# Joined query products carried one group further, into the seventh sequence of an eight-sequence attention and expert block

## The chip, the cores and the metric

The kernel runs on one core of one Trainium2 chip. The metric is device time in microseconds (us) of one execution; several executions are given by their median. Five engines work side by side, each in its own program order: PE (TensorE, matrix products), DVE (VectorE), ACT (ScalarE), POOL (GpSimd) and SP, which here only issues DMAs. They wait for each other through semaphores.

## What is computed

The input x holds 8 sequences of 512 rows of 256 numbers, all in float32. The block is

```python
x = x + _layernorm(_L0_attn_ref(_layernorm(x), wq, bq, wkv, bkv, wo))
x = x + _layernorm(_L0_ffn_ref(_layernorm(x), ...))
```

The attention has 4 groups of 4 query heads (head size 128), each group with one key and one value head, a sinusoidal position table added to queries and keys, a causal mask and a softmax. The second half is a mixture of 64 experts (6 per row, at most 64 rows for an expert) with a shared expert beside it. The queries of one group of one sequence, which the change is about, are

```python
q = (x @ wq + bq).reshape(b, t, G, QPG, D).transpose(0, 2, 3, 1, 4)
q = q + pe
```

so for one group a product of 512 x 256 rows with 256 x 512 weights.

## The kernel before

The attention is a loop over `k` from 0 to 127, here called *places*. Place k belongs to sequence b = k // 16 and, in it, to slot s = k % 16; four places make a group. The sequences are counted from 0 in the code, so the seventh sequence is b = 6, whose places are 96 to 111, and the sixth sequence's slot 11 is place 91. The order of the instructions on every engine is the order in which the program writes them (a manual schedule), so one late instruction holds up everything behind it on its engine.

At each place PE makes four blocks of scores (L566; at most three lie in PSUM at a time, in the pool `ps_s`), DVE masks them and takes their minimum (L570), ACT takes the exponential (L574), DVE the reciprocal of the sums (L580), and POOL scales the weights with it (L584, `weigh`). One place later DVE transposes the weights in blocks (L602, `turned`), four DMAs write them to HBM (`ex_d`, L606) and one reads them back in another order (`et`, L612). Two places after the scores, `mix` multiplies them with the values (L639), and ACT brings the result out (`ao`, L650). Projections of earlier places run between these (`projections`, L664 or, in sequences 1 to 5, sums of blocks: `cross` on POOL, L707 to L710, whose result `across` multiplies at L716). Keys and values of the next group are made at L377 and L388. The rows of the sequences b = 1 to 6 are transposed through HBM, and POOL sorts them into `xnt` (L364, `sort`).

Queries are made in two ways. `queries(k)` (L426, result added up at L431) makes two heads of half of a group's rows in four products of 256 columns; a group takes four such calls, sixteen products, and eight DVE instructions. Groups 2 to 23 (group = 4 b + g) are instead made in pairs by seven products of summed blocks for what eight plain ones would give: `ask(k)` (four products, L490 to L493), `answer` (one), `ask_rest` (one) and `ask_fourth` (one), all recorded at L470. They take from POOL four sums of the weights (`join_heads`, once for each group of heads, at the start) and four sums of the rows (`join_rows`, L459 to L462, once per sequence, into the one tile `rows_joined`), and eight DVE instructions for each `ask`, sixteen a group (L496, L497, L505, L510, L515). `ask(k)` runs at even k for the group k // 4 + 1, two calls a group, and its parts are spread over places k, k + 1 and k + 2. Its two PSUM banks come from the pool `ps_m` of three; the bank `back` is given up only at place k + 2, by `answer_fourth`. Which groups are made so is decided by `in_pairs`:

```python
def in_pairs(k):
    return k % 2 == 0 and JOINED_FROM <= k // QPG + 1 < JOINED_TO
```

and the plain way begins where it ends:

```python
asked_for = {2: (4, 5), 3: (6,), 4: (7,)}.get(k, (k + 2,) if JOINED_TO * QPG <= k + 2 < NK else ())
```

So before the change `queries(96)` to `queries(99)`, for group 24, run at places 94 to 97, and `queries(100)` at place 98. The tile that takes the queries is tagged `qt` in the plain way, and in the pairs `qt` for odd groups and `rows` for even ones.

From place 94 on the experts run beside the attention (`routed`): first a table is built (`tables`, DVE sorting steps at L804 and L806 and two small products, L883 and L895), from place 97 on rows are gathered by POOL (L948) and weights loaded by DMAs that ACT issues (L958, L965). Place 97 also has `combine`, six POOL sums (L744 to L749), and place 98 `cross(47)` and `across(47)`.

## Time and profile before

| what | number |
|---|---|
| three executions | 1351.22, 1346.76, 1350.15 us, median 1350.15 |
| the profiled execution | 1346.28 us |
| its span on the core | 1344.6 us, so 1.7 us lie around it |
| PE busy | 1319.8 us, 98% of the span |
| DVE, POOL, ACT busy | 911.5, 660.3, 546.8 us |
| granted clock of PE | 0.997 of full speed |
| plain query products, L426 | 40 calls of `queries`, 8 records of 379 ns each |
| joined query products, L470 | 44 calls of `ask`, 14 records each |

A product of float32 is two records on PE, so four products of `queries` are eight records. The records overlap: one of 256 columns is listed at 379 ns, while the next starts about 217 ns after it (4 records in 0.87 us, 8 in 1.73 us). The start-to-start time is what a product costs in a stream, and "busy" alone does not tell whether PE is held up. Times "at" a number are us from the start of the span. Place 92 has its scores at 841.63, place 93 at 852.44, then 859.99, 868.56, 876.96, 884.62 (place 97), 894.16 (place 98) and 906.60 (place 99).

### The profile page before, as it was taken

What the parts mean: (1) busy time and instruction counts of PE and PEld (TensorE: products, weight loads), DVE (VectorE), ACT (ScalarE), POOL (GpSimd) and SP (SyncE); (2) the same over time, 40 slices, a digit from 0 to 9 for tenths busy, and PEclk for the clock granted to TensorE, in tenths of its full rate; (3) what the DMA queues carried; (4) which work ended last, traced back from release to release, by engine and by line L of the source; (5) the groups of instructions that cost most, each with busy time, mean ns of one, the idle gap of its engine ahead of it and who ended that gap; (6) DMA issues with size and microseconds to landing.
All of it is one profiled execution on the core that took longest, in us unless ns stands there. A gap on an engine that the chain in (4) does not pass through costs nothing. (4 is left out here: it accounts for less than half of the span.)

```text
span 1344.6 us, 21778 instructions
## 1 busy us (share of the span) xinstructions
PE 1319.8 (98%) x6746; PEld 1018.7 (76%) x6746; DVE 911.5 (68%) x2931; ACT 546.8 (41%) x1665; POOL 660.3 (49%) x1080
## 2 busy tenths in 40 slices
PE   9999999999999999999999999999999999999997
PEld 7877887888778887788778877876667676767774
DVE  5575577777887678777886778666656444567645
ACT  3333354334443454344433443434343334444523
POOL 4556463436452563446434643355545444477711
PEclk9999999999999999999999999999999999999999
DMA  8676677756775676566765667579999889777712
GB/s 268 176 219 208 201 215 219 205 185 211 220 218 174 201 226 213 177 209 204 224 193 162 204 189 202 171 213 303 307 284 281 246 239 299 182 239 262 234 36 72
DMA packets 160435, 285.53 MB, mean 212 GB/s; under 512 B 17292, under 2 KB 123437, under 8 KB 160317
## 3 DMA queue, kind: packets, MB, share of 16 engines
q1 hardware_dynamic: 122893, 212.14, 52.6%
q0 software_dynamic: 13328, 36.05, 9.1%
q10 hardware_dynamic: 24096, 35.92, 8.5%
q8 instruction: 55, 0.90, 0.3%
q14 instruction: 63, 0.52, 0.1%
HBM read 168.44 MB, written 115.61 MB: 211 GB/s over the span
## 5 line engine op out<-in xcount | busy, mean ns | idle before, releaser
L584 POOL TENSOR_SCALAR e<-e,recip 128x512 f32<-128x512 f32 (+1 forms) x504 | 245.3, 525 | 424.1 <-DVE recip L580 367.7
L574 ACT ACTIVATE e<-e,least 128x32 f32<-128x32 f32 (+1 forms) x504 | 258.5, 514 | 260.4 <-DVE least L570 235.1
L639 PE MATMUL pav<-et,v 128*128 128x256 f32 x1280 | 300.4, 382 | 11.5 <-DMA et<-ex_d 8.9
L639 PEld LDWEIGHTS pav<-et,v 128*128 128x128 f32 x1280 | 241.5, 191 | 52.8 <-issue 7.1
L566 PE MATMUL psc<-kt,qt 128*128 128x32 f32 (+15 forms) x1024 | 274.9, 407 | 0.9 <-DVE qt L431 0.4
L570 DVE CUSTOM_DVE_ANT_0 e<-psc,mask 128x32 f32<-128x32 f32 (+1 forms) x504 | 204.2, 430 | 96.4 <-PE psc L566 93.8
L650 ACT ACTIVATE ao<-pav,bv_sb 128x256 f32<-128x256 f32 x255 | 107.1, 471 | 368.5 <-PE pav L639 344.7
L566 PEld LDWEIGHTS psc<-kt,qt 128*128 128x128 f32 x1024 | 161.5, 191 | 59.4 <-issue 25.9
L602 DVE STREAM_TRANSPOSE eb<-e 128x1024 f32<-128x1024 f32 (+1 forms) x252 | 197.5, 822 | 2.0 <-POOL e L584 1.5
L1021 POOL DMA_INDIRECT y_d<-dd,idx x32 | 51.1, 1597 | 93.2 <-ACT e L574 27.2
L574 ACT ACTIVATION_READ_ACCUMULATOR e<-e,least 128x1 f32 x504 | 94.6, 188 | 0.0
L716 PEld LDWEIGHTS pc<-set,crossed 128*128 128x128 f32 x640 | 77.0, 192 | 4.9 <-issue 1.7
L716 PE MATMUL pc<-set,crossed 128*128 128x128 f32 x640 | 78.8, 276 | 0.6 <-POOL crossed L710 0.6
L426 PE MATMUL pq<-xnt,wq_sb 128*128 128x256 f32 x320 | 75.5, 380 | 0.0
L716 PEld LDWEIGHTS ps<-set,ao 128*128 128x128 f32 x480 | 59.9, 192 | 15.3 <-issue 7.4
L470 PE MATMUL pq_back<-rows_joined,heads 128*128 128x256 f32 x264 | 71.3, 379 | 0.0
L388 PEld LDWEIGHTS pv<-wkv_sb,xnt 128*128 128x128 f32 x512 | 65.9, 192 | 4.5 <-issue 1.1
L388 PE MATMUL pv<-wkv_sb,xnt 128*128 128x128 f32 x512 | 67.5, 275 | 0.5 <-ACT ao L650 0.5
L426 PEld LDWEIGHTS pq<-xnt,wq_sb 128*128 128x128 f32 x320 | 59.2, 190 | 9.2 <-issue 0.7
L379 DVE SCALAR_TENSOR_TENSOR kt<-pk,bk_sb,pe_sb 128x512 f32<-128x512 f32 x32 | 24.0, 750 | 60.5 <-PE pk L377 58.5
L470 PEld LDWEIGHTS pq_back<-rows_joined,heads 128*128 128x128 f32 x264 | 50.2, 190 | 16.2 <-issue 8.2
L377 PE MATMUL pk<-xnt,wkv_sb 128*128 128x512 f32 x128 | 60.2, 593 | 0.3 <-ACT xnt L120 0.3
(281 smaller groups left out, 2017.6 us busy)
## 6 DMA issues: line engine op xcount, KB each, us to landing
ex_d<-eb SPq DMA_DIRECT2D x504, 160.0 KB
et<-ex_d SPq DMA_DIRECT2D x126, 640.0 KB
wgu<-in_w_gate ACTq DMA_DIRECT2D x32, 352.0 KB
wgu<-in_w_up ACTq DMA_DIRECT2D x32, 352.0 KB
wd<-in_w_down ACTq DMA_DIRECT2D x32, 352.0 KB
set<-wc_d SPq DMA_DIRECT2D x20, 512.0 KB
set<-ws_d SPq DMA_DIRECT2D x20, 384.0 KB
y<-y_d POOLq DMA_DIRECT2D x10, 512.0 KB, 6.8
```

What stands on the lines that cost most here:

```text
L377: nc.tensor.matmul(pk, lhsT=wkv_sb[:, c, g, 0, :], rhs=s["xnt"][:, c, :], start=c == 0, stop=c == NC - 1)
L388: nc.tensor.matmul(pv[:, i, :], lhsT=s["xnt"][:, c, ts(2 * n + i, P)], rhs=wkv_sb[:, c, g, 1, :], start=c == 0, stop=c == NC - 1, skip_gro ...
L426: nc.tensor.matmul(pq[:, n, :, :], lhsT=wq_sb[g][:, c, ts(2 * pair + n, D)], rhs=seqs[b]["xnt"][:, c, :].rearrange("p (u v) -> p u v", v=P ...
L470: nc.tensor.matmul(out, lhsT=factor[0], rhs=factor[1], start=first, stop=last, skip_group_check=True)
L566: nc.tensor.matmul(psc[:, :w], lhsT=halves[k // 2][:, at, :, :].rearrange("d h t -> d (h t)"), rhs=seqs[b]["kt"][g][:, :w], start=True, st ...
L570: nc.vector.tensor_tensor_reduce(out=e, in0=psc[:, :w].rearrange("p (c t) -> p c t", t=BS), in1=mask[:, T - w :].rearrange("p (c t) -> p c ...
L574: nc.scalar.activation(e, e, AF.Exp, bias=l["least"][:, q : q + 1], scale=-1.0, accum_out=l["total"][:, q : q + 1])
L584: engine.tensor_scalar(e, e, recip[:, q : q + 1], 1.0, ALU.mult, ALU.mult)
L602: nc.vector.transpose(eb[:, :, first : first + count, :, :].rearrange("p a j r t -> p j a r t"), weighed[k % 2][:, end - count : end, :, : ...
L639: nc.tensor.matmul(pav[n // NI][:, :, n % 2, :], lhsT=seqs[b]["v"][g][:, j, :], rhs=et[:, :, first + j, :], start=j == 0, stop=j == count ...
L650: nc.scalar.activation(ao, pav[n // NI][:, :, n % 2, :], AF.Identity, bias=bias)
L716: nc.tensor.matmul(bank_[:, n, :], lhsT=a, rhs=w, start=pair == 0 and n == 0, stop=pair == 1 and n == len(factors[0]) - 1, skip_group_chec ...
```

## The change

The bound of the joined groups goes from 24 to 25, and `join_rows` is called at slot 11 of the sixth sequence (b = 5) too.

```diff
-JOINED_FROM, JOINED_TO = 2, (EARLY + 1) * G
+JOINED_FROM, JOINED_TO = 2, (EARLY + 1) * G + 1
...
-            if k == 2 or s == 11 and b < EARLY:
+            if k == 2 or s == 11 and b <= EARLY:
                 join_rows(b + 1 if s == 11 else 0)
```

With EARLY = 5 and G = 4 the first line reads 2, 25. The calls `queries(96)` to `queries(99)` at places 94 to 97 go. `ask(92)` comes at place 92 (behind the projection there) and `ask(94)` at place 94 (in front of `weigh`, as at every even place of the sixth sequence but 92), with their answers at places 93 to 96. The four POOL sums of the seventh sequence's rows come at the end of place 91. The queries of group 24 lie in tiles tagged `rows` instead of `qt`; `load_whole_again` takes a `rows` tile at place 98. The sums of the weights that group 24 reads lie in tiles tagged `wgu` and `wd`, into which the experts' weights are loaded from places 97 and 98 on. No DMA is added, removed or moved in the program's order, and no line number changes.

## The prediction

> **What bounds the kernel now.** I read the page first. PE is busy in every slice, and the granted clock is 0.997, so the kernel ends when PE has worked through its stream; a change counts by what it does to that stream.

> ```profile
> PE 1319.8 (98%) x6746; PEld 1018.7 (76%) x6746; DVE 911.5 (68%) x2931; ACT 546.8 (41%) x1665; POOL 660.3 (49%) x1080
> PE   9999999999999999999999999999999999999997
> ```

> "Busy" has modelled ends, so next I read the timeline of PE at places 94 to 98, start to start (start, duration, engine, line, operation, count, and in brackets the idle time before it and what ended it).

> ```profile
> 872.18 1.89 PE L426 MATMUL pq<-xnt,wq_sb 128*128 128x256 f32 x8
> 873.91 2.32 PE L639 MATMUL pav<-et,v 128*128 128x256 f32 x10
> ...
> 888.56 1.89 PE L426 MATMUL pq<-xnt,wq_sb 128*128 128x256 f32 x8
> 890.28 2.32 PE L639 MATMUL pav<-et,v 128*128 128x256 f32 x10
> ...
> 897.49 1.89 PE L426 MATMUL pq<-xnt,wq_sb 128*128 128x256 f32 x8
> 900.00 2.05 PE L716 MATMUL pc<-set,crossed 128*128 128x128 f32 x16 [0.61 <-POOL crossed L710]
> ```

> The reader is to see two things. One call of `queries` costs 873.91 - 872.18 = 1.73 us. And PE runs without a gap from place 92 on until 900.00, where it waits for POOL. So I read POOL there:

> ```profile
> 889.77 1.89 POOL L584 TENSOR_SCALAR e<-e,recip 128x448 f32<-128x448 f32 x4 [6.16 <-DVE recip L580]
> 891.83 1.08 POOL L948 DMA_INDIRECT gx<-xg_d,idx  x1 [0.17 <-issue]
> 892.94 0.46 POOL L744 TENSOR_TENSOR o<-partial 128x128 f32<-128x128 f32 x1
> ...
> 896.01 1.00 POOL L948 DMA_INDIRECT gx<-xg_d,idx  x1
> 897.03 0.74 POOL L707 TENSOR_TENSOR crossed<-ao 128x256 f32<-128x256 f32 x1
> ...
> 899.22 0.73 POOL L710 TENSOR_TENSOR crossed<-ao,crossed 128x256 f32<-128x256 f32 x1
> ```

> From 889.77 to 899.95 POOL has 10.2 us of work without a pause: `weigh(97)`, a gather, the six sums of `combine`, a gather, `cross(47)`. It starts from DVE's reciprocal, which follows the scores of place 97 (884.62). So PE's product at 900.00 stands 15.38 us behind the scores of place 97 by POOL's chain, whatever PE does in between, as long as that is less. This is the heart of the forecast.

> **PE's own work.** Removed: four `queries`, 4 x 1.73 = 6.92 us, one each at places 94 to 97. Added: where the fifth sequence does the same an `ask` takes 1.73 us (697.17 to 698.90) and each of its three later products 0.43 (for instance 710.37 to 710.80); 1.73 + 3 x 0.43 = 3.02, twice 6.04 us. By place: 92 +1.73; 93 +1.29; 94 none (1.73 for 1.73); 95 1.29 - 1.73 = -0.44; 96 and 97 each -1.73. If every record counted: 6.04 - 6.92 = -0.9 us. Until the scores of place 97, however, all of the new work is done and only three of the four removals: 6.04 - 5.19 = **+0.85**. The fourth, at 888.56, lies inside POOL's 15.38 us. Removing it lets PE come 1.73 us earlier to a place where it waits already, so the wait of 0.61 becomes about 2.3 (1.4, if item 4 below takes its part) and the end does not move.

> **Waits that the change adds before place 97.** Between 841 and 899 PE has no idle time that could be filled or freed, so none of these can be below zero.

> 1. Place 92 to 93. DVE gets the four instructions of `ask` in front of its sorting steps (L804, L806): 0.42 + 0.42 + 0.48 + 0.42, spaced 0.33 apart in the earlier slots, about 1.65 us from 851.35. The sorting then ends near 855.65, while the moved scores of place 93 come at 854.17; the fourth score block needs the first one's bank, which DVE frees near 855.9, at PE's 855.85. Cost 0.1 (0 to 1.0, the whole lag of DVE).
> 2. Place 94. `pm` (L883) now takes the third PSUM bank beside the two of `ask(94)`, so `mix(92)` waits until DVE has emptied `front`. There this is 2.22 us after the first product (697.17 to 699.39); PE arrives after 1.73 + 0.26 = 1.99. Cost 0.25 (0 to 0.5, the wait of PE for ACT in front of L388 near 800).
> 3. Place 96. The landing marks put `et` of place 94 at 880.23, 11.67 us after the scores of place 95; PE will want it 8.40 - 0.44 + 3.45 = 11.41 us after them. Cost 0.25 (0 to 1.8, the longest wait for an `et` near by, at 929.5).
> 4. Place 97. `et` of place 95 lands at 887.81, 10.85 us after the scores of place 96. PE wants it at 13.32 now and at 13.32 - 2 x 1.73 = 9.86 then: a wait of 1.0 us, but it lies inside POOL's 15.38 (4.9 + 2.2 + 1.7 + 2.0 + 1.3 + 1.7 = 13.8 us of PE). Cost 0.

> So the scores of place 97 come 0.85 + 0.1 + 0.25 + 0.25 = about **1.5 us later**, and all behind them with them.

> **At no cost, and their cover.** POOL's four sums: 4 x 0.72 = 2.9 us at the end of place 91, from 836.92, where POOL sits idle 4.21 us until `ao` at 841.13. The fourth must wait for a product at 840.31 to 840.7 that reads the old sum, so `cross(44)` starts some 0.6 late; its reader is PE at 854.33, ten us on. Without that cover they would cost 2.9. DVE's sixteen instructions for eight are 16 x 0.44 - 8 x 0.475 = +3.2 us in five places whose DVE is 51 to 88% busy; beyond items 1 and 2 the waits of DVE for PE in front of each place (0.98 at 860.20, 0.82 at 869.14) take them. No queue gets a new DMA. The reload into `rows` at place 98 waits for scores of place 97, by then done; the weight tiles tagged `wd` are reloaded at 907.73, 30 us behind their last new reader.

> [...]

> **Behind place 98.** The experts' loads are issued by ACT behind `mix(95)`, which comes about 0.7 us earlier in its place than before. PE's next waits are for `et`, 1.80 at 929.52 and 1.00 at 944.25, amid a DMA share of 0.98. They could vanish (-2.8) or double (+2.8). I take 0: loads and exchange move together.

> **The sum.** 1346.28 + 1.5 = 1347.8 for the profiled execution. That one lies 3.9 us below the median of the three runs, so the forecast for the median is 1350.15 + 1.5 = **1351.7**.

> **The rivals.**

> *A, every record counts.* POOL's chain gives way: the gathers or `combine` start earlier, or the 0.61 was chance. Then -0.9: 1349.3. For it speaks that PE is 98% busy; against it the unbroken POOL rows. With the two `et` waits gone, too, 1346.5.

> *B, slower: the exchange falls behind the weight stream.* From 906 on each place loads over 2 MB of weights; an `et` that landed 3.9 us after issue at 883.94 took 7.0 at 922.34. If the shifted loads get ahead of the exchange, the two waits double: 1.5 + 2.8 = +4.3, 1354.5. It decides once an `ex_d` or `et` is issued behind one more 0.7 MB pair of loads than now. For it: the DMA share; against it: the loads are issued in place order and the `et` of place 96 begins to land at 896.3 and is wanted at 901.89.

> *C, DVE sets the pace at 92 to 96.* Items 1 and 3 at their upper ends: 0.85 + 1.0 + 0.5 + 1.8 = +4.15, 1354.3, by gaps before 885. Against it: DVE's idle time in front of every place.

> **Chances.** Forecast 0.62, A 0.2, B 0.12, C 0.06. What a measurement can tell from no change is 0.3%, 4.05 us; the four executions lie between 3.9 below and 1.1 above the median. B and C lie just past 4.05 (0.14 of their 0.18), and scatter adds 0.03 from the forecast: slower 0.17. Scatter takes A below -4.05 rarely (0.04) and the forecast more rarely (0.02): faster 0.06. The rest, 0.77, is no change. The range goes from A with its waits gone to B and C with a little scatter: 1346.3 to 1355.

> **What would show it.** Right: no L426 record between 863 and 897; POOL's L707 at place 98 still ends an unbroken row that began at L584; in front of that `pc` a PE wait of 1.3 to 2.3 us instead of 0.61; a wait of about 1 us for `et` at place 97; the scores of place 97 some 1.5 us later. Wrong: that `pc` less than 15 us behind the scores of place 97 (A), `et` waits over 4 us in sum between 905 and 950 (B), PE gaps over 2 us in sum before place 97 (C).

## The result, and the profile after

The changed kernel took 1353.35 us in the median of seven runs (1350.99 to 1357.57), the kernel before 1346.89 beside it (seven, 1345.42 to 1351.22): a ratio of 1.0045 [1.0027, 1.0062], some 6 us slower. In a second comparison with more runs (the first experiment) it was 1.003 [1.0014, 1.0046], 4 us. The forecast was +1.5 us, a ratio of 1.0011, which both intervals exclude. The predicted range held the time, and the direction of the sum was right; its size was not, and the loss stands at or just over the 0.3% that was called no change (a greater loss had been given 0.17). That the time itself came within 1.7 us of the forecast 1351.7 is luck: the three runs of the kernel before on which that rests had a median 3.3 us above that of the seven, from which the same sum gives 1348.4, 5 us short of what was measured.

The profiled execution of the changed kernel is its slowest one: 1357.57 us, span 1355.7, granted clock 0.993. A profile of the same kernel taken later has a span of 1349.2. Wherever a number below hangs on one execution, both are given.

The page of the changed kernel, PE's row and its 40 slices:

```profile
PE 1325.1 (98%) x6742; PEld 1022.1 (75%) x6742; DVE 914.1 (67%) x2939; ACT 546.3 (40%) x1665; POOL 662.9 (49%) x1084
PE   8999999999999999999999999999999999999997
```

PE has four records less (6746 - 32 + 28) and is as busy as before: still the engine that sets the end.

**Up to place 98.** The timeline of PE, places 94 to 98 of the changed kernel:

```profile
867.57 1.03 PE L470 MATMUL pq_front<-xnt,wq_sb 128*128 128x256 f32 x4
...
869.89 2.40 PE L639 MATMUL pav<-et,v 128*128 128x256 f32 x10 [0.16 <-PE pm L883]
...
887.20 2.31 PE L566 MATMUL psc<-kt,qt 128*128 128x96 f32 x8
889.35 1.95 PE L716 MATMUL pc<-set,crossed 128*128 128x128 f32 x16
892.37 2.43 PE L639 MATMUL pav<-et,v 128*128 128x256 f32 x10 [1.08 <-DMA et<-ex_d]
...
902.57 2.05 PE L716 MATMUL pc<-set,crossed 128*128 128x128 f32 x16 [0.99 <-POOL crossed L710]
```

No L426 stands between 863 and 897 any more. At place 97 (scores at 887.20) PE waits 1.08 us for `et`, and at place 98 again 0.99 us for POOL; that is what removing `queries(99)` bought. (Removing `queries(98)`, which lies ahead of these scores, did count: the shift of the scores falls from 3.41 at place 96 to 1.97 at place 97.) POOL there:

```profile
892.35 1.89 POOL L584 TENSOR_SCALAR e<-e,recip 128x448 f32<-128x448 f32 x4 [4.72 <-DVE recip L580]
894.40 1.08 POOL L948 DMA_INDIRECT gx<-xg_d,idx  x1 [0.17 <-issue]
895.51 0.46 POOL L744 TENSOR_TENSOR o<-partial 128x128 f32<-128x128 f32 x1
...
898.59 1.00 POOL L948 DMA_INDIRECT gx<-xg_d,idx  x1 [0.16 <-issue]
899.61 0.74 POOL L707 TENSOR_TENSOR crossed<-ao 128x256 f32<-128x256 f32 x1
...
901.79 0.73 POOL L710 TENSOR_TENSOR crossed<-ao,crossed 128x256 f32<-128x256 f32 x1
```

The row is as unbroken as before, 10.2 us from 892.35 to 902.52, and PE's `pc` starts at its end: 15.37 us behind the scores of place 97, where it was 15.38. The wait in front of it, 0.99, is below the 1.3 to 2.3 that the forecast gave as a sign: the wait for `et` at place 97 and the slower start of the products behind it (`pc` and `mix` took 5.29 us from their start to that of `pk`, where they had taken 1.79 + 2.16) took about 1.3 of the 1.73 us and left 0.4. The scores of place 99 come at 909.17 instead of 906.60. Place 90 already lies 0.61 us later in this execution, for reasons ahead of the change, so the change itself is worth +1.97 there, and +2.05 in the second profile of the same kernel.

**Behind place 98** the two profiles part. The view of PE's waits, 905 us to 1340 us (total, times, longest), first before, then after:

```profile
PE pav L639 <- DMA et<-ex_d: 8.0, 6, 2.8
```

```profile
PE pav L639 <- DMA et<-ex_d: 11.3, 6, 2.9
```

PE waits for the same thing in both kernels, the exchange of weights, and some 3 us longer after. The same view of the later profile gives 8.9 in 5 waits, only 0.9 more than before, although its span is 4.6 us longer than that of before. So there is a cost that the waits do not show. The windows of the changed kernel (start and end, length, busy us and records of PE, of its weight loads, DVE, ACT, POOL, then the granted clock, DMA share, GB/s):

```profile
1185.00:1195.00 10.00, 10.00 (x42) 7.58 (x42) 6.85 (x25) 3.19 (x10) 8.23 (x14) 1.00 0.92 306
1195.00:1205.00 10.00, 7.21 (x29) 5.82 (x28) 5.47 (x21) 1.75 (x6) 6.49 (x11) 0.83 0.93 310
1268.00:1275.50 7.50, 5.18 (x26) 3.45 (x24) 4.11 (x16) 1.64 (x5) 5.54 (x10) 1.00 0.77 224
1275.50:1283.00 7.50, 6.90 (x18) 5.54 (x19) 1.84 (x10) 2.26 (x6) 2.09 (x4) 0.55 0.54 199
```

and two products of its timeline there:

```profile
1200.34 4.10 PE L639 MATMUL pav<-et,v 128*128 128x256 f32 x10 [2.79 <-DMA et<-ex_d]
...
1276.10 4.61 PE L639 MATMUL pav<-et,v 128*128 128x256 f32 x10 [2.92 <-DMA et<-ex_d]
```

The ten records take 4.10 and 4.61 us instead of 2.43 at 892.37. The clock column says why: in the two stretches that hold them, behind waits of 2.79 and 2.92 us, the granted clock was 0.83 and 0.55; it was 0.5 for 3.41 us from 1200.35 and for 6.83 us from 1275.44. The kernel before has the first of the two (0.83 from 1195 to 1205); in its profile the waits near 1270 are 0.38 and 0.82 us, and the granted clock from 1268 to 1276 was 1.00:

```profile
1195.80 3.95 PE L639 MATMUL pav<-et,v 128*128 128x256 f32 x10 [2.78 <-DMA et<-ex_d]
...
1268.72 2.40 PE L639 MATMUL pav<-et,v 128*128 128x256 f32 x10 [0.38 <-DMA et<-ex_d]
...
1275.50 2.43 PE L639 MATMUL pav<-et,v 128*128 128x256 f32 x10 [0.82 <-DMA et<-ex_d]
```

### The profile page after: what moved, and what is told of

Its sections match the earlier page's. It is cut to its first block, busy times and chain, and to the rows that moved or that the text cites. A ratio compares the mean times of both kernels' runs of the same rounds, so it can differ in the third digit from the quotient of the medians.

```text
span 1355.7 us, 21785 instructions
## 1 busy us (share of the span) xinstructions
PE 1325.1 (98%) x6742; PEld 1022.1 (75%) x6742; DVE 914.1 (67%) x2939; ACT 546.3 (40%) x1665; POOL 662.9 (49%) x1084
## 3 DMA queue, kind: packets, MB, share of 16 engines
q1 hardware_dynamic: 122893, 212.14, 52.7%
q0 software_dynamic: 13328, 36.05, 8.9%
## 5 line engine op out<-in xcount | busy, mean ns | idle before, releaser
L584 POOL TENSOR_SCALAR e<-e,recip 128x512 f32<-128x512 f32 (+1 forms) x504 | 245.2, 525 | 425.4 <-DVE recip L580 367.2
L639 PE MATMUL pav<-et,v 128*128 128x256 f32 x1280 | 304.6, 386 | 15.8 <-DMA et<-ex_d 12.8
L639 PEld LDWEIGHTS pav<-et,v 128*128 128x128 f32 x1280 | 244.4, 193 | 57.9 <-issue 10.2
L716 PEld LDWEIGHTS pc<-set,crossed 128*128 128x128 f32 x640 | 77.0, 192 | 4.8 <-POOL crossed L710 1.4
L716 PE MATMUL pc<-set,crossed 128*128 128x128 f32 x640 | 78.9, 277 | 1.0 <-POOL crossed L710 1.0
L470 PE MATMUL pq_back<-rows_joined,heads 128*128 128x256 f32 x276 | 74.6, 379 | 0.0
L716 PEld LDWEIGHTS ps<-set,ao 128*128 128x128 f32 x480 | 59.9, 192 | 15.3 <-issue 6.9
L388 PEld LDWEIGHTS pv<-wkv_sb,xnt 128*128 128x128 f32 x512 | 65.9, 192 | 4.5 <-issue 1.1
L388 PE MATMUL pv<-wkv_sb,xnt 128*128 128x128 f32 x512 | 67.5, 276 | 0.5 <-ACT ao L650 0.5
L426 PE MATMUL pq<-xnt,wq_sb 128*128 128x256 f32 x288 | 67.8, 379 | 0.0
L716 PE MATMUL ps<-set,ao 128*128 128x128 f32 x480 | 60.1, 275 | 0.0
```

The source lines that it names most:

```text
L388: nc.tensor.matmul(pv[:, i, :], lhsT=s["xnt"][:, c, ts(2 * n + i, P)], rhs=wkv_sb[:, c, g, 1, :], start=c == 0, stop=c == NC - 1, skip_gro ...
L426: nc.tensor.matmul(pq[:, n, :, :], lhsT=wq_sb[g][:, c, ts(2 * pair + n, D)], rhs=seqs[b]["xnt"][:, c, :].rearrange("p (u v) -> p u v", v=P ...
L470: nc.tensor.matmul(out, lhsT=factor[0], rhs=factor[1], start=first, stop=last, skip_group_check=True)
L584: engine.tensor_scalar(e, e, recip[:, q : q + 1], 1.0, ALU.mult, ALU.mult)
L639: nc.tensor.matmul(pav[n // NI][:, :, n % 2, :], lhsT=seqs[b]["v"][g][:, j, :], rhs=et[:, :, first + j, :], start=j == 0, stop=j == count ...
L716: nc.tensor.matmul(bank_[:, n, :], lhsT=a, rhs=w, start=pair == 0 and n == 0, stop=pair == 1 and n == len(factors[0]) - 1, skip_group_chec ...
```

## The experiments

There were twelve runs. "Local shift" is when the scores of place 99 come against the profile of before, with the offset at place 90 taken off. The theories in the expectations go by letters. In short: S blames the tiles in which group 24's queries lie; M is the forecast, a local delay carried to the end one for one; D is a delay that grows on its way; E places the extra loss at places 118 to 127, where the exchange meets the reading back of `y` for the last step of the earlier sequences; F places it at 98 to 102, among the experts' weight loads.

**1. The changed kernel again (`after_again`).** No edit.

> The changed kernel unchanged, for a second profile. Theory M (about 2 us are made at places 92 to 97 by PE's own work, the moved waits and POOL's chain; the rest comes behind place 98, where a wait for et that grows past about 2.5 us is followed by 3.4 us at half the PE clock): the scores of place 98 again 1.5 to 2.0 us late against their position in the kernel before, counted from place 90; the waits for et at places 100 to 102 differ from the first profile; ratio 1.003 to 1.006. Theory S (the other tiles for the queries of group 24 change later waits for good): the same, but with the extra time behind place 98 at the same places and of the same size as in the first profile.

Measured: 1354.06 us (twelve runs, 1348.31 to 1358.49) beside 1349.38, ratio 1.003 [1.0014, 1.0046]; local shift +2.05. The loss and the local shift are real. The wait of 2.46 us at 947.03 in the first profile did not come again.

**2. The kernel before again (`before_again`).** No edit.

> The kernel before unchanged, for a second profile and to see how its waits behind place 98 vary. Theory M: waits for et at other places or of other sizes than in the first profile, by 1 to 3 us; ratio 0.998 to 1.002. Theory S: the same waits within 0.5 us.

Measured: 1348.68 us, 0.9995 [0.9983, 1.0008]; no local shift (0.01), but 1.89 us earlier at place 102. So places 100 to 103 move by some two microseconds from run to run without any edit, and one profile cannot tell there.

**3. Only the tiles (`tag_only`).** The kernel before, with the queries of group 24 in the tiles that the change gives them.

```diff
-halves[half] = p2.tile([D, 2 * NI, QPG, BS], F32, tag="qt", name=f"qt_{half}")
+halves[half] = p2.tile([D, 2 * NI, QPG, BS], F32, tag="rows" if half in (48, 49) else "qt", name=f"qt_{half}")
```

> The kernel before, the queries of group 24 made the plain way but put into tiles tagged rows as in the change. Theory M: ratio 1.000, within 0.2%. Theory S: ratio 1.002 to 1.004, the part of the change's loss that lies behind place 98.

Measured: 1348.72 us, 0.9991 [0.9975, 1.0007], local shift 0.01. S falls.

**4. The changed kernel, POOL's `combine(5, 0)` moved from place 97 to behind `cross(47)` at place 98 (`after_cross_first`).** The point is whether POOL's row holds PE at 902.57.

```diff
             if b in CROSSED and not odd:
                 cross(j)
+                if last and b == EARLY:
+                    combine(b, 0)
...
-                if n == 2 * G - 2 and odd:
+                if n == 2 * G - 2 and odd and b < EARLY:
                     combine(b, 0)
```

> The changed kernel with the six POOL sums of combine, 3.0 us, moved from the end of place 97 to behind cross(47) at place 98. Theory M: POOL's row from weigh(97) to cross(47) is 3.0 us shorter, the 1.0 us wait of PE in front of the product at L716 at place 98 goes, and the removal at place 97 counts: the scores of place 99 come 1.0 us earlier than in the change, ratio to the kernel before 1.001 to 1.005. If POOL's chain isn't what holds PE there, nothing moves.

Measured: 1352.91 us, 1.0019 [1.0004, 1.0034]. Its PE timeline at places 97 and 98:

```profile
890.98 2.43 PE L639 MATMUL pav<-et,v 128*128 128x256 f32 x10 [0.73 <-DMA et<-ex_d]
...
898.30 1.89 PE L426 MATMUL pq<-xnt,wq_sb 128*128 128x256 f32 x8
900.03 1.95 PE L716 MATMUL pc<-set,crossed 128*128 128x128 f32 x16
```

and its POOL (L950 is the gather, two lines further down than before):

```profile
894.76 0.98 POOL L950 DMA_INDIRECT gx<-xg_d,idx  x1 [0.30 <-issue]
895.76 0.75 POOL L707 TENSOR_TENSOR crossed<-ao 128x256 f32<-128x256 f32 x1
...
897.97 0.73 POOL L710 TENSOR_TENSOR crossed<-ao,crossed 128x256 f32<-128x256 f32 x1
898.65 0.46 POOL L744 TENSOR_TENSOR o<-partial 128x128 f32<-128x128 f32 x1
```

POOL ends `cross(47)` at 898.70, ahead of PE, whose wait is gone: `pc` follows the queries without a gap. The local shift falls from 2.0 to 0.37, by 1.6 us where 1.0 was expected. So it is POOL's row that held PE, and the fourth removed `queries` begins to count only when that row gives way. Rival A is refuted for the kernel as it is. In this profile 1.1 us of the gain is lost again before place 100, in a wait in front of `pd`, a product of the experts (L1012 here, two lines further down than before):

```profile
917.39 1.08 PE L1012 MATMUL pd<-wd,ht 88*64 88x256 f32 x8 [1.06 <-DVE tables L936]
```

The order of POOL's sums does not decide on it: `before_cross_first` (run 7), with the same order, has no such wait, and `before_again`, without an edit, has one of 0.65.

**5. A plain delay (`delay5`).** The kernel before, with five products at place 92 that nobody reads: 2.17 us of PE, about the local shift of the change, and nothing else of it.

```diff
+            if k == 92:
+                extra = ps_s.tile([P, 2, P], F32, tag="s", name="extra")
+                for n in range(5):
+                    nc.tensor.matmul(extra, lhsT=wq_sb[0][:, 0, :P], rhs=seqs[5]["xnt"][:, 0, :2 * P], start=True, stop=True)
```

> The kernel before with five more products of 256 columns at place 92, whose result nobody reads: 10 records, 2.17 us of PE, nothing else. Theory M (a delay made at places 92 to 97 is carried to the end one for one): the scores of places 93 to 99 2.2 us late, ratio 1.0016, within 0.0010 to 1.0022 counted as 1.0010 to 1.0022. Theory D (a delay there makes the waits for et behind place 98 and the half clock after them worse): ratio 1.003 or more. Theory K (it is absorbed in the waits for et at places 100 and 101): ratio 1.000 to 1.0007.

Measured: 1349.06 us beside 1348.13, 1.0012 [0.9991, 1.0032]; local shift 2.17. The interval takes in both 2 and 4 us, so the ratio alone decides nothing; in the table of means below it has 2.1 us once the halved clock is counted apart, good to about 1 us.

**6. Only POOL's sums (`rows_only`).** The kernel before, with `join_rows` at slot 11 of the sixth sequence.

```diff
-            if k == 2 or s == 11 and b < EARLY:
+            if k == 2 or s == 11 and b <= EARLY:
```

> The kernel before with the four POOL sums at the end of place 91 alone; what they make is not read. All theories: cross(44) 0.5 us late, no score moved by 0.1 us, ratio 0.999 to 1.001.

Measured: 1348.44 us, 1.0001 [0.9982, 1.002]. No score moves at place 99 (0.00). Its POOL at place 91:

```profile
837.18 0.73 POOL L461 TENSOR_TENSOR rows_joined<-xnt 128x256 f32<-128x256 f32 x1
839.85 0.72 POOL L462 TENSOR_TENSOR rows_joined<-xnt,rows_joined 128x256 f32<-128x256 f32 x1 [1.95 <-PE pq_back L470]
840.54 0.72 POOL L707 TENSOR_TENSOR crossed<-ao 128x256 f32<-128x256 f32 x1
```

The fourth sum waits 1.95 us for the product that still reads the old one, `cross(44)` starts some 0.6 late as forecast, and nobody is late for it.

**7. The kernel before with `combine` behind `cross` (`before_cross_first`).** The edit of run 4 on the kernel before.

> The kernel before with the six POOL sums of combine moved behind cross(47) at place 98. Theory M: the 0.61 us wait of PE in front of L716 at place 98 goes and no more, the scores of place 99 0.6 us earlier, ratio 0.9990 to 1.0000. If the order of these sums costs something by itself behind place 98 (combine's result or the scaling of the weights of place 98 late), ratio 1.001 to 1.002.

Measured: 1347.58 us, 0.9987 [0.9967, 1.0007], local shift -0.88, where -0.6 was expected. It is not shown to beat the kernel before.

**8. The change without its waits (`after_all`).** Run 4, and `pm` in a bank of the pool `ps_s`, and one of the two sorting rounds of place 92 moved to place 93.

```diff
-            pm = bank([NX, CAP], "pm")
+            pm = ps_s.tile([NX, CAP], F32, tag="s", name="pm")
...
                     steps["6D"] = steps.pop("6M")
+                    steps |= {"12D": go("r"), "13D": go("r", 3)}
```

> The changed kernel with three waits taken away: one of DVE's two sorting steps moved from place 92 to place 93, the tile pm put into the pool of the scores instead of the pool of ask's banks, and combine moved behind cross(47). Theory M: of the 2.0 us made before place 99 the waits of 0.5, 0.3 and 1.6 go, so the scores of place 99 come 0.3 to 0.6 us earlier than in the kernel before; ratio 0.9985 to 1.0005. If what is lost lies behind place 98 and has another cause than the delay: ratio 1.0015 to 1.003 in spite of it.

Measured: 1350.97 us, 1.0015 [0.9999, 1.003]; local shift -0.56. The scores of place 94 come +3.03 later, which is 1.73 + 1.29 and 0.01, where the changed kernel has +3.64. In its timeline the scores of place 93 have no gap, and `mix(92)` no wait:

```profile
855.54 2.06 PE L566 MATMUL psc<-kt,qt 128*128 128x96 f32 x8
...
869.80 2.43 PE L639 MATMUL pav<-et,v 128*128 128x256 f32 x10
```

The local loss is gone, even a little is gained, and the kernel is still not faster. The interval takes in no loss at all, so this run alone proves little, but it suggests that part of the loss does not come from the local delay and arises behind place 98. The means below bear that out.

**What the profiles of these runs show behind place 98.** First the shift of the scores, in us:

| place | after | after_again | after_cross_first | after_all | delay5 | before_again | tag_only | rows_only | before_cross_first |
|---|---|---|---|---|---|---|---|---|---|
| 99 | 1.97 | 2.05 | 0.37 | -0.56 | 2.17 | 0.01 | 0.01 | 0.00 | -0.88 |
| 100 | 1.97 | 2.05 | 1.50 | -0.56 | 2.17 | 0.73 | 0.54 | 0.00 | -0.88 |
| 102 | 3.85 | -0.72 | -0.41 | -3.15 | 0.44 | -1.89 | -0.43 | -2.77 | -1.80 |
| 118 | 3.92 | -0.74 | 0.06 | -1.47 | 0.97 | -1.01 | 0.02 | -2.43 | -1.83 |
| 125 | 4.23 | -1.85 | 1.91 | -2.45 | 1.52 | -2.63 | 0.12 | -2.09 | -1.81 |
| 126 | 8.94 | 3.21 | 6.29 | 3.19 | 5.24 | 1.61 | 0.19 | -2.26 | -0.87 |
| 127 | 8.72 | 2.85 | 5.20 | 2.65 | 4.15 | 0.52 | 0.33 | -2.21 | -1.10 |

Between places 103 and 118 a shift changes by 0.5 at most. From 125 to 126 alone the four profiles with the change lose 4.4 to 5.6 us, but `before_again` 4.2 and `delay5` 3.7 too; the three others lose 0.9 or less. PE's waits for `et` there, and the stretches of halved clock behind place 117 (in units of 3.41 us; a halved unit costs 1.7):

| kernel | place 118 | 121 | 122 | 125 | 126 | 127 | halved |
|---|---|---|---|---|---|---|---|
| before | 2.8 | | 1.2 | 0.4 | 0.8 | | 1 |
| tag_only | 2.7 | | 1.0 | 0.4 | 1.0 | 0.4 | 1 |
| rows_only | 2.6 | | 0.3 | 0.2 | 0.9 | | 1 |
| before_cross_first | 2.9 | 0.8 | | 1.3 | 0.6 | 0.6 | 1 |
| before_again | 2.2 | 1.0 | | 2.9 | | 1.6 | 1 |
| delay5 | 3.1 | 1.2 | | 2.4 | | 1.7 | 2 |
| after | 2.8 | 1.2 | | 2.9 | | 1.3 | 3 |
| after_again | 3.1 | 1.1 | | 3.3 | | 1.2 | 2 |
| after_cross_first | 4.3 | 0.6 | | 3.1 | | 1.3 | 3 |
| after_all | 3.0 | 1.1 | | 3.9 | | 2.6 | 3 |

There are two patterns. In one PE waits at place 122 and little at 125; in the other at 121, and then 2.4 to 3.9 us at 125, mostly with a halved clock behind it. (`before_cross_first` lies between them, with 0.8 and 1.3.) The profiles of kernels without the change show both, the four with it only the costly one. From about 945 us on, place 101, PE's records and the DMAs that SP issues are the same in before and after and come in the same order, and the kernel before shows both patterns without an edit; so it is timing that picks the pattern.

Then the mean over all timed runs, each group beside its own runs of the kernel before. "Halved" is (1 - granted clock) x span, "rest" the span without it:

| kernel, runs | span | halved | rest | local shift |
|---|---|---|---|---|
| after_again, 12 | +3.5 | +0.9 | +2.6 | +2.0 |
| after_cross_first, 12 | +2.9 | +1.0 | +1.9 | +0.4 |
| after_all, 12 | +2.1 | +1.7 | +0.4 | -0.6 |
| before_again, 12 | -0.9 | 0.0 | -0.9 | 0.0 |
| tag_only, 12 | -1.5 | -0.1 | -1.4 | 0.0 |
| rows_only, 12 | -0.1 | +0.4 | -0.5 | 0.0 |
| delay5, 12 | +1.7 | -0.4 | +2.1 | +2.2 |
| before_cross_first, 12 | -0.8 | +0.3 | -1.0 | -0.9 |

Single runs scatter by 2 to 3.7 us (standard deviation), so a mean of twelve is good to 0.6 to 1.1 us. In the five kernels without the change the span is 1.5 us below to 0.1 us above what the local shift alone gives: within the scatter that is M. In the three with it the rest is 0.6 to 1.6 us over the local shift and the halved clock takes 0.9 to 1.7 us more: together 1.5 to 2.7 us that the local account does not have, and above all five of the others.

**9 to 12. Without the last step of the first five sequences (`before_nofin`, `after_nofin`, `after_all_nofin`, `before_cross_nofin`).** These kernels do not write the output of the first five sequences. If E is right, leaving that step out takes the extra loss away and leaves the local shift.

```diff
                     if first <= n <= first + 3 if mixed else n in (first, first + 2):
-                        next(rows[b])
+                        pass
```

> The kernel before without the last step of sequences 0 to 4: the reading back of y_d and x1_d, the norm and the writing of the output (finish_early) are left out, and with them the transfers that share the queues with the exchange at places 117 to 126. It is the base for the other three of this call. All theories: the waits for et of places 119 to 125 and the half clock near 1270 go, 2 to 8 us faster than the kernel before.

> The changed kernel without the last step of sequences 0 to 4, as in before_nofin. Theory E (what is lost over the 2.0 us of places 92 to 97 is lost at places 119 to 126, where the exchange meets those transfers, and in the half clock behind it): 1.5 to 2.5 us slower than before_nofin. Theory F (it is lost at places 98 to 102, among the weight loads): 3 to 5 us slower than before_nofin.

> The changed kernel with the three waits taken away, without the last step of sequences 0 to 4. Theory E: from 1.0 us faster to 0.5 us slower than before_nofin, by the scores of place 99, which came 0.56 us earlier. Theory F: 1 to 3 us slower than before_nofin.

> The kernel before with combine behind cross(47), without the last step of sequences 0 to 4. Theory E: 0.5 to 1.2 us faster than before_nofin, by the scores of place 99, which came 0.88 us earlier. Theory F: within 1.5 us of before_nofin on either side.

Measured, six runs each: 1338.39, 1340.51, 1338.58 and 1339.31 us; against the whole kernel before 0.9928 [0.9901, 0.9955], 0.9935 [0.9909, 0.9961], 0.9926 [0.9898, 0.9955] and 0.993 [0.9904, 0.9956]. PE's waits for `et` from 905 us to 1330 us in `before_nofin` and in `after_nofin`:

```profile
PE pav L639 <- DMA et<-ex_d: 2.3, 3, 1.2
```

```profile
PE pav L639 <- DMA et<-ex_d: 2.6, 3, 1.2
```

Eight and eleven microseconds of waiting have become two and a half in both, and in none of the four profiles is the clock halved before the last 8 us. `before_nofin` is some 10 to 12 us faster than the kernel before, more than the 2 to 8 expected. The transfers that are left out were not in the queue of the exchange, as the expectation had it: q0 moved 25.57 MB instead of 36.05, q1 212.14 in both. The step that is left out is more than its transfers, and these runs do not separate the two. The change now costs 2.1 us by medians, 1.5 by mean spans (its local shift here is +2.19), and without its waits +0.2 or 0.0. In `after_nofin` the shift grows no more from place 112 to 127 (2.45, 2.57). This speaks for E and against F, whose places are still in these kernels with all their weight loads. It is no exact account: the intervals overlap one another, and `before_cross_nofin`, with a local shift of -0.88, came out 0.9 slower in the median, where E had it 0.5 to 1.2 faster and F's range holds it (in its profile the shift is +0.24 one place later, behind a wait of 1.05 us like that of run 4).

## Why the prediction was right in its mechanism and wrong in its sum

**PE's own work, +0.85 until place 97, the fourth removal swallowed by POOL: right.** The steps between scores show it: +1.73 at place 93, and with the waits taken out of the change (run 8) +1.29 at place 94. POOL's 15.38 us came out as 15.37, and run 4 showed that it is this row which holds PE.

**Item 1, DVE's sorting in front of place 93, forecast 0.1: under-sized.** It cost 0.6, by the scores of place 94 in the changed kernel (+3.64) against run 8 (+3.03, so 0.61 to 0.62):

```profile
854.77 1.31 PE L566 MATMUL psc<-kt,qt 128*128 128x96 f32 x6
856.43 1.02 PE L566 MATMUL psc<-kt,qt 128*128 128x448 f32 x2 [0.34 <-DVE least L570]
```

DVE was on time: it gave the bank up for 856.43, where the forecast, with the 0.61 added, had 856.5. PE was early. I had it come to the fourth block 1.68 us behind the first; in the records of before that is 853.58 - 852.44 = 1.14. The missing 0.5 is this one slip.

**Item 2, `pm`'s bank, forecast 0.25: right** (0.20 by the scores of place 95, with 0.16 listed as a wait). **Item 3, `et` at place 96, forecast 0.25: right** (0.3 by the scores of place 97). **Item 4, `et` at place 97, forecast 1.0 and hidden: right** (1.08, and hidden by POOL). The scores of place 97 came +1.97 instead of +1.5; the 0.5 is item 1.

**What was called free was free.** Run 6 shows it for POOL's sums, run 3 for the tiles.

**The step that failed: "Behind place 98. ... I take 0: loads and exchange move together."** Up to there the sum was 0.5 us short. Behind it the kernels with the change lost another 1.5 to 2.7 us in the mean, 20 places on, where I had not looked: runs 9 to 12 point to the stretch where the last step of the earlier sequences runs, places 118 to 127, where PE waits 2 to 4 us at a time for the exchange, and behind some of these waits the clock was halved (behind 2.92 us at 1276.10 in the changed kernel, not behind 3.06 us at 1195.43 in `after_again`). I had quoted the granted clock of 0.997 as a sign of health and did not ask where the missing 0.003, or 4 to 5 us, lay (1.7 us of it behind the wait at place 118, the rest in the last 6 us). Rival B had the right kind of mechanism, an exchange that lands later, but the wrong place. Its own sign, `et` waits over 4 us between 905 and 950, did not show (3.0 us in the first profile, 0.3 in the second).

**What stays open** is why every one of the four profiles with the change fell into the costly pattern, `after_all` too, whose scores at place 99 are earlier than before. In the profiles the two patterns differ in when SP issues `et` of place 119 against POOL's reads of `y`: in the profile of before 0.2 us behind one and 1.3 ahead of the next, in that of after 1.2 behind one and 0.4 ahead of the next. It then lands 4.7 and 6.4 us after its issue. All ten profiles sort by this. The three that issue it 0.2 to 0.4 us behind the read (`before`, `tag_only`, `rows_only`) have it land in 4.2 to 5.9 us, and PE does not wait for it at place 121; the other seven issue it 0.55 to 1.2 us behind, it lands in 6.0 to 6.9, and PE waits 0.6 to 1.2 us. That this order is the cause, and that the wait at place 125 follows from it, is still argued, not shown; no run moved it alone. A lucky draw of four profiles is not excluded either, and over the timed runs it is a matter of odds: a granted clock of 0.998 or more came in 6 of the 43 runs of the three kernels with the change, against 29 of 81 of the kernel before.

## What to carry to other kernels

Count records only up to the next point that a chain on another engine paces: what was removed inside that chain here, 1.73 us, bought waits of 1.08 and 0.99 where one of 0.61 had stood, and what was added before it was paid in full (2.17 us of products in run 5, scores 2.17 later). Then go through the rest of the kernel for waits of an otherwise busy PE that are a few microseconds long, however far from the edit, since kernels that lay within some 3 us of one another at place 99 here waited 0.2 to 3.9 us at place 125, and a halved clock, 1.7 us a unit, came on top in some. A change of 0.2% in a kernel whose runs scatter by 0.2% needs a dozen runs and a second profile before any difference behind the edit is explained.

## What the runs showed of the hardware that was not expected

**What a halved stretch costs.** The records of `mix` then started 427 ns apart instead of 217, so by these two numbers one unit of 3.41 us did half the work and cost 1.7 us on top of the wait that went before it.
